# Fetching one edge tile in forty row by row from SyncE and ScalarE in a relational graph network on one core

## The chip, the cores and the metric

The program runs on one core of a Trainium2 chip. The metric is the time of one execution on the device in microseconds (us). The kernel before the change was run three times: 4817.36, 4808.80 and 4808.24 us, median 4808.8 us. The first of these runs is the profiled one.

The engines are called by the profile's names: PE (TensorE, the matrix unit; PEld is its loading of weights), DVE (VectorE), ACT (ScalarE), POOL (GpSimd) and SP (SyncE). SP, ACT and POOL each have a queue from which they issue transfers (DMAs).

## The reference

A graph has 12,500 nodes with 128 features each and 200,000 edges, sorted by destination. The relation of an edge is the place of the greatest of ten numbers in its attributes. A layer takes, for every destination node and every relation, the mean of the features of the source nodes, multiplies each mean by that relation's 128x128 matrix, adds over the relations, and adds a dense term of the node's own features:

```python
def _rgcn_layer(x, src, dst, edge_type, w_rel, root, bias):
    seg = dst * NUM_REL + edge_type
    xs = x[src]
    sums = segment_sum(xs, seg, N * NUM_REL)
    cnt = segment_sum(ones, seg, N * NUM_REL)
    mean = (sums / maximum(cnt, 1.0)[:, None]).reshape(N, NUM_REL, -1)
    return einsum('nrd,rdo->no', mean, w_rel) + x @ root + bias

edge_type = argmax(msg[:, 16:-16], axis=1)
h = relu(_rgcn_layer(x, src, dst, edge_type, w_rel1, root1, b1))
out = layernorm(x + _rgcn_layer(h, src, dst, edge_type, w_rel2, root2, b2))
```

So both layers have to fetch, for each of the 200,000 edges, a row of 128 floats (512 bytes) that an index picks from a table in device memory: the input `x` in the first layer, the hidden table `hD` in the second.

## The kernel before, in words

**Tiles, quads, groups.** The edges are cut into 1563 tiles of 128. Four tiles (`Q`) make a quad and sixteen (`G`) a group, so a layer has 391 quads and 99 groups (the last ones are shorter).

**One quad** (`edges`). POOL fetches the rows of four tiles with one indirect DMA each into a buffer `g` (`gather`, L352); the pool of these buffers has `RING = 22` slots, so POOL can be 22 quads, 88 tiles, ahead. For each tile, DVE builds a matrix `oh` (L366) that holds an edge's weight at the column of its destination and relation, out of 12 destinations by 10 relations, and PE multiplies the rows by it into the accumulator memory `zp` (L368; three buffers of one quad). ACT copies a full `zp` to `zs` (L369; two buffers of one group). DVE has twelve buffers for `oh`.

**One group.** When the four quads of a group are in `zs`, PE multiplies them by the ten relation matrices into `po` (L373), for which there is one buffer (`ps_o`, `bufs=1`). DVE loads the sixteen first destinations into registers, four with one load (L376), and adds each tile's twelve columns to the accumulator `acc` at an address from a register (L381).

**What runs between the quads.** After each quad the function `between` is called. In the first layer it advances the preparation of the next chunks of 128 tiles: types, keys, and `count`, which counts for every edge the edges with the same key among its neighbours at up to `L = 40` places. `count` loads the keys with their neighbours into `kh`, copies them with ACT into accumulator memory as `kp` (L255; pool `ps_k`, one bank), and then compares, for each of 40 distances, a slice of `kp` with a slice of `kh` on DVE (L259), 40 comparisons for a chunk and 13 chunks. PE adds up the results (L260, L261).

**Blocks.** Whenever the groups have passed the end of 512 nodes, `finish` completes that block: `hidden` in the first layer, `final` in the second. Their loads and stores go by SP (`rows_dma`, L287).

**Order.** The program is unrolled. A planner draws up one list for each engine, and an engine works its list in order. A wait stands before the instruction that needs it, so all that is queued on that engine behind a waiting instruction waits too.

Of the kernel before, what the change touches and what calls it, by code (L numbers as in the profile page):

```python
# [9 lines left out]
F32 = mybir.dt.float32  # L10
BF16 = mybir.dt.bfloat16
I32 = mybir.dt.int32
AF = mybir.ActivationFunctionType
ALU = mybir.AluOpType
AX = mybir.AxisListType
PSUM = bass.MemoryType.PSUM
DRAM = bass.MemoryType.DRAM
DVE = mybir.EngineType.DVE
SP = mybir.EngineType.SP

P = 128
NREL = 10
# [3 lines left out]
KW = NREL * WN  # L26
Q = 4
G = 16
RING = 22
L = 40  # L30
CT = 128
YB = 512
# [8 lines left out]
def rgcn_resnorm_kernel(ctx: ExitStack, tc: tile.TileContext, x, src, dst, attr, w_rel1, root1, b1,  # L41
# [13 lines left out]
    nc = tc.nc  # L55
    N, C = x.shape
    E = src.shape[0]
    D = attr.shape[1]
    CE = CT * P
    NT = -(-E // P)  # L60
# [16 lines left out]
    fast = ctx.enter_context(ExitStack())  # L77
# [2 lines left out]
    msgp = fast.enter_context(tc.tile_pool(name="msgp", bufs=2))  # L80
    eqp = fast.enter_context(tc.tile_pool(name="eqp", bufs=6))
    gpool = fast.enter_context(tc.tile_pool(name="gpool", bufs=RING))
    dpool = fast.enter_context(tc.tile_pool(name="dpool", bufs=12))
    zpool = fast.enter_context(tc.tile_pool(name="zpool", bufs=2))
    ps_z = fast.enter_context(tc.tile_pool(name="ps_z", bufs=3, space=PSUM))
    ps_o = fast.enter_context(tc.tile_pool(name="ps_o", bufs=1, space=PSUM))
    ps_k = fast.enter_context(tc.tile_pool(name="ps_k", bufs=1, space=PSUM))
    ps_c = fast.enter_context(tc.tile_pool(name="ps_c", bufs=1, space=PSUM))

    ident = const.tile([P, P], F32, name="ident")  # L90
# [1 line left out]
    idxE = keep.tile([P, NCH * CT], I32, name="idxE")  # L92
# [3 lines left out]
    def chunk_rows(c):  # L96
        return min(CT, NT - c * CT)
# [11 lines left out]
    def to_edges(to, t, c):  # L109

        p = chunk_rows(c)
        pt = ps_c.tile([P, P], F32, name="pt")
        nc.tensor.transpose(pt[:, :p], t[:p], ident[:p, :p])
        nc.vector.tensor_copy(to[:, c * CT:c * CT + p], pt[:, :p])
# [130 lines left out]
    def count(c):  # L245

        p = chunk_rows(c)
        n = p - 1 if c == NCH - 1 else p
        kh = prep.tile([P, P + 2 * L], F32, name="kh")
        nc.sync.dma_start(kh[:n], bass.AP(KD.tensor, KD.offset + c * CE, [[P, n], [1, P + 2 * L]]))  # L250
        if n < p:
            nc.sync.dma_start(kh[n:p], bass.AP(KD.tensor, KD.offset + E - P, [[P, 1], [1, P + 2 * L]]))
        yield
        kp = ps_k.tile([P, P + 2 * L], F32, name="kp")
        nc.scalar.activation(kp[:p], kh[:p], AF.Copy)  # L255
        pc = ps_c.tile([P, P], F32, name="pt")
        for d in range(1, L + 1):
            eq = eqp.tile([P, P + L], BF16, name="eqb")
            nc.vector.tensor_tensor(eq[:p, :P + d], kp[:p, L - d:L + P], kh[:p, L:L + P + d], op=ALU.is_equal)  # L259
            nc.tensor.matmul(pc[:p], identb[:p, :p], eq[:p, :P], start=(d == 1), stop=False)  # L260
            nc.tensor.matmul(pc[:p], identb[:p, :p], eq[:p, d:d + P], start=False, stop=(d == L))  # L261
            if d % 2 == 0:
                yield
        wp = prep.tile([P, P], F32, name="wp")
        nc.vector.tensor_scalar(wp[:p], pc[:p], 1.0, None, op0=ALU.add)
        nc.vector.reciprocal(wp[:p], wp[:p])
        if c == NCH - 1:
            nc.vector.tensor_tensor(wp[:p], wp[:p], own[:p], op=ALU.mult)
        to_edges(wE, wp, c)
        yield  # L270
# [75 lines left out]

    HELD = "clamped to a node on the chip"

    def gather(table, t0, n):
        g = gpool.tile([P, Q, C], F32, name="g")  # L350
        for j in range(n):
            nc.gpsimd.indirect_dma_start(out=g[:, j, :], out_offset=None, in_=table,  # L352
                                         in_offset=bass.IndirectOffsetOnAxis(ap=idxE[:, t0 + j:t0 + j + 1], axis=0))
        return g

    def edges(table, l, t0, n, between):

        zs = zpool.tile([P, NREL, G, WN], F32, name="zs")
        for q in range(0, n, Q):
            m = min(Q, n - q)  # L360
            g = gather(table, t0 + q, m)
            zp = ps_z.tile([P, Q, KW], F32, name="zp")
            for j in range(m):
                t = t0 + q + j
                oh = dpool.tile([P, KW], F32, name="oh")
                nc.vector.tensor_scalar(oh, iota[:, :KW], keyE[:, t:t + 1], wE[:, t:t + 1], op0=ALU.is_equal,  # L366
                                        op1=ALU.mult)
                nc.tensor.matmul(zp[:, j, :], g[:, j, :], oh, start=True, stop=True)  # L368
            nc.scalar.activation(zs[:, :, q:q + m, :], zp[:, :m].rearrange("c j (r n) -> c r j n", n=WN), AF.Copy)  # L369
            between()  # L370
        po = ps_o.tile([P, G, WN], F32, name="po")
        for r in range(NREL):
            nc.tensor.matmul(po[:, :n], wsb[l][:, r, :], zs[:, r, :n], start=(r == 0), stop=(r == NREL - 1))  # L373
        for j0 in range(0, n, 4):
            m = min(4, n - j0)
            _, offs = nc.values_load_multi_w_load_instructions(  # L376
                bt[0:1, t0 + j0:t0 + j0 + m], engines=[DVE], min_val=0, max_val=N - 1,
                skip_runtime_bounds_check_because=HELD)
            for j in range(m):
                s = ds(offs[j], WN)  # L380
                nc.vector.tensor_tensor(acc[:, s], acc[:, s], po[:, j0 + j], op=ALU.add)  # L381

    def groups():
        t = 0
        while t < NT:
            n = min(G, NT - t)
            if n < G and n > 4:
                n = 8 if n > 8 else 4
            yield t, n
            t += n  # L390

    def layer(table, l, finish, steps):

        done = 0
        for t0, n in groups():
            def between():
                while steps:
                    till, left, s = steps[0]
                    k = max(1, -(-left[0] * Q // max(Q, till - t0)))
                    for _ in range(k):  # L400
                        left[0] -= 1
                        if next(s, steps) is steps:
                            steps.pop(0)
                            break
                    break
            edges(table, l, t0, n, between)
            while done < NBLK and (t0 + n >= NT or t0 + n >= (done + 1) * (YB // 8) + SLACK):
                finish(done)
                done += 1
# [5 lines left out]
    def as_steps(f, c):  # L415
        f(c)
        yield
# [5 lines left out]
    for _ in count(0):  # L423
        pass
    todo = []
    for c in range(1, NCH):
        s = [as_steps(sources, c + 1), types(c + 1)] if c + 1 < NCH else []
        todo.append((c * CT - 8, [8 + L // 2 + 2], chain(*s, count(c))))
    layer(x, 0, hidden, todo)
    layer(hD, 1, final, [])  # L430

    pf = ps_f.tile([P, YB], F32, name="pf")
# [19 lines left out]
    def each_tile(before, stages):  # L452

        with tc.For_i(0, E, GT) as e:
# [29 lines left out]
            nw = nc.values_load(bw[0:1, 1:2], min_val=1, max_val=-(-N // W), skip_runtime_bounds_check_because=HELD)  # L484
            b0 = nc.values_load(bw[0:1, 0:1], engines=[DVE, SP], min_val=0, max_val=N - 1,
                                skip_runtime_bounds_check_because=HELD)
# [109 lines left out]
```

## Time and profile before

| | |
|---|---|
| median of three runs | 4808.8 us |
| the profiled execution | 4817.36 us, of it the span of the engines 4815.5 us |
| POOL | busy 2971.9 us (62%), 3126 gathers |
| PE / PEld | busy 2439.3 us (51%) / 2184.5 us (45%) |
| DVE | busy 1585.0 us (33%) |
| ACT | busy 470.9 us (10%) |
| mean granted TensorE clock | 0.706 |
| mean traffic | 58 GB/s |

The span falls into four parts: some 110 us in which the first chunks are prepared while POOL is gathering already; the first layer to about 2346 us; a short change of tables, in which POOL waits 74.2 us for the last rows of `hD`; and the second layer to the end. A busy share is an average over all of it. "Idle before" in a row of the profile is the time in which an engine stood still just before instructions of that group, with the releaser that ended most of it; "issue" is time in which it waited for nothing that the profile shows, "remote" a release whose sender it does not show. Issuing a transfer and loading or computing an address in a register are work of an engine's sequencer and are not in its busy time.

### The profile page before, as it was taken

What the parts mean: (1) busy time and instruction counts of PE and PEld (TensorE: products, weight loads), DVE (VectorE), ACT (ScalarE), POOL (GpSimd) and SP (SyncE); (2) the same over time, 40 slices, a digit from 0 to 9 for tenths busy, and PEclk for the clock granted to TensorE, in tenths of its full rate; (3) what the DMA queues carried; (4) which work ended last, traced back from release to release, by engine and by line L of the source; (5) the groups of instructions that cost most, each with busy time, mean ns of one, the idle gap of its engine ahead of it and who ended that gap; (6) DMA issues with size and microseconds to landing.
All of it is one profiled execution on the core that took longest, in us unless ns stands there. A gap on an engine that the chain in (4) does not pass through costs nothing.

```text
span 4815.5 us, 44360 instructions
## 1 busy us (share of the span) xinstructions
PE 2439.3 (51%) x12272; PEld 2184.5 (45%) x12272; DVE 1585.0 (33%) x7623; ACT 470.9 (10%) x899; POOL 2971.9 (62%) x3136
## 2 busy tenths in 40 slices
PE   0456655655655565665615444444444444444456
PEld 0445554545555455555514443444444444444445
DVE  3333443344334333333302222232222322232234
ACT  0001110111011111111100100000000000000001
POOL 6566666666666666666266666666666666666661
PEclk9766676676767676666756677777777776776777
DMA  5121222122122221112111221112111211121110
GB/s 163 41 75 51 79 76 75 53 76 75 51 80 74 56 55 52 50 51 54 32 48 46 55 53 49 49 52 55 50 51 51 57 51 50 50 56 49 51 52 25
DMA packets 180408, 279.04 MB, mean 58 GB/s; under 512 B 55448, under 2 KB 127015, under 8 KB 177031
## 3 DMA queue, kind: packets, MB, share of 16 engines
q0 software_dynamic: 100032, 205.07, 16.2%
q1 hardware_dynamic: 76957, 69.59, 4.6%
q8 instruction: 108, 1.77, 0.2%
q10 hardware_dynamic: 3168, 1.44, 0.1%
q14 instruction: 143, 1.17, 0.1%
HBM read 262.28 MB, written 13.60 MB: 57 GB/s over the span
## 4 chain that ended last, share of the span: by engine, by line
PE 29%; issue 27%; another core or an unknown queue 24%; DVE 8%; POOL 7%; ACT 2%; DMA 1%; DVEq 1%; SPq 0%; ACTq 0%; POOLq 0%
PE zp L368 14%; PE po L373 12%; POOL g L352 7%; DVE oh L366 4%; DVE acc L381 3%; ACT zs L369 1%; PE pf L303 1%; PE pt L261 1%; PE pt L260 1%; PE pf L302 1%; DMA g<-in_x_dram,idxE 1%; DVEq L376 1%; ACT fT L299 0%; PE pf L297 0%
## 5 line engine op out<-in xcount | busy, mean ns | idle before, releaser
L352 POOL DMA_INDIRECT g<-hD,idxE x1563 | 1477.4, 945 | 946.9 <-issue 429.4
L368 PE MATMUL zp<-oh,g 128*128 128x120 f32 x6252 | 1269.8, 364 | 1551.8 <-issue 1001.8
L352 POOL DMA_INDIRECT g<-in_x_dram,idxE x1563 | 1493.2, 955 | 802.9 <-issue 416.1
L368 PEld LDWEIGHTS zp<-oh,g 128*128 128x128 f32 x6252 | 1134.9, 267 | 1675.4 <-issue 1105.0
L366 DVE TENSOR_SCALAR oh<-iota,keyE,wE 128x120 f32<-128x120 f32 x3126 | 1028.5, 351 | 675.4 <-remote 340.8
L381 DVE TENSOR_TENSOR acc<-acc,po 128x12 f32 x3126 | 518.1, 166 | 2032.6 <-remote 1268.1
L373 PE MATMUL po<-zs,w 128*128 128x192 f32 x3960 | 916.7, 386 | 439.6 <-issue 225.3
L373 PEld LDWEIGHTS po<-zs,w 128*128 128x128 f32 x3960 | 807.2, 232 | 507.5 <-issue 301.7
L369 ACT ACTIVATE zs<-zp 128x480 f32<-128x480 f32 (+1 forms) x782 | 417.8, 570 | 3650.1 <-remote 2408.5
L259 DVE TENSOR_TENSOR eqb<-kp,kh 128x129 bf16<-128x129 f32 (+43 forms) x520 | 148.4, 305 | 196.5 <-remote 145.3
L260 PE MATMUL pt<-eqb,identb 128*128 128x128 bf16 (+1 forms) x520 | 120.9, 269 | 160.0 <-issue 130.7
L261 PE MATMUL pt<-eqb,identb 128*128 128x128 bf16 (+1 forms) x520 | 121.6, 275 | 52.6 <-issue 49.7
L261 PEld LDWEIGHTS <-identb 128*128 128x128 bf16 (+1 forms) x520 | 62.8, 121 | 176.2 <-issue 170.3
L302 PE MATMUL pf<-root,fT 128*128 128x128 f32 x392 | 105.3, 359 | 55.9 <-issue 41.0
L303 PE MATMUL pf<-ident,a 128*128 128x128 f32 x392 | 107.4, 365 | 13.9 <-issue 8.1
L302 PEld LDWEIGHTS pf<-root,fT 128*128 128x128 f32 x392 | 84.3, 263 | 63.9 <-issue 48.0
L260 PEld LDWEIGHTS <-identb 128*128 128x128 bf16 (+1 forms) x520 | 66.8, 129 | 75.4 <-issue 74.9
L303 PEld LDWEIGHTS pf<-ident,a 128*128 128x128 f32 x392 | 88.2, 270 | 22.5 <-issue 14.5
L299 ACT ACTIVATE fT<-pf 128x512 f32<-128x512 f32 (+1 forms) x50 | 29.3, 587 | 498.7 <-remote 245.3
L332 DVE TENSOR_TENSOR v<-pf,xb 128x512 f32<-128x512 f32 (+2 forms) x26 | 17.1, 660 | 174.7 <-remote 127.3
L297 PE MATMUL pf<-ident,hb 128*128 128x128 f32 x98 | 21.9, 356 | 23.9 <-DVE v L332 17.6
L342 DVE TENSOR_SCALAR o<-v,mv,rstd 128x128 f32<-128x128 f32 x98 | 27.8, 349 | 0.2
(71 smaller groups left out, 371.6 us busy)
## 6 DMA issues: line engine op xcount, KB each, us to landing
m<-in_edge_attr_dram SPq DMA_DIRECT2D x24, 1344.0 KB
g<-in_x_dram,idxE POOLq DMA_INDIRECT x1563
g<-hD,idxE POOLq DMA_INDIRECT x1563
xb<-in_x_dram SPq DMA_DIRECT2D x48, 256.0 KB
hD<-hb SPq DMA_DIRECT2D x24, 256.0 KB
hb<-hD SPq DMA_DIRECT2D x24, 256.0 KB
out_dram<-o SPq DMA_DIRECT2D x24, 256.0 KB
w<-in_L_gnn_w_rel_dram ACTq DMA_DIRECT2D x2, 640.0 KB
```

The source lines that it names most:

```text
L259: nc.vector.tensor_tensor(eq[:p, :P + d], kp[:p, L - d:L + P], kh[:p, L:L + P + d], op=ALU.is_equal)
L260: nc.tensor.matmul(pc[:p], identb[:p, :p], eq[:p, :P], start=(d == 1), stop=False)
L261: nc.tensor.matmul(pc[:p], identb[:p, :p], eq[:p, d:d + P], start=False, stop=(d == L))
L302: nc.tensor.matmul(pr[:h, t, :], fT[:, t * P:t * P + h], rsb[l], start=True, stop=False)
L303: nc.tensor.matmul(pr[:h, t, :], a[:, t * P:t * P + h], ident, start=False, stop=True)
L352: nc.gpsimd.indirect_dma_start(out=g[:, j, :], out_offset=None, in_=table, in_offset=bass.IndirectOffsetOnAxis(ap=idxE[:, t0 + j:t0 + j + ...
L366: nc.vector.tensor_scalar(oh, iota[:, :KW], keyE[:, t:t + 1], wE[:, t:t + 1], op0=ALU.is_equal, op1=ALU.mult)
L368: nc.tensor.matmul(zp[:, j, :], g[:, j, :], oh, start=True, stop=True)
L369: nc.scalar.activation(zs[:, :, q:q + m, :], zp[:, :m].rearrange("c j (r n) -> c r j n", n=WN), AF.Copy)
L373: nc.tensor.matmul(po[:, :n], wsb[l][:, r, :], zs[:, r, :n], start=(r == 0), stop=(r == NREL - 1))
L376: _, offs = nc.values_load_multi_w_load_instructions(bt[0:1, t0 + j0:t0 + j0 + m], engines=[DVE], min_val=0, max_val=N - 1, skip_runtime_b ...
L381: nc.vector.tensor_tensor(acc[:, s], acc[:, s], po[:, j0 + j], op=ALU.add)
```

## The change

Of every 80 tiles, one is now fetched by SP and one by ACT in place of POOL. The first layer's SP tiles are 79, 159, ..., ACT's 119, 199, ..., nineteen each in a layer. For such a tile the 128 indices are first loaded into one partition (`sr`); then, eight rows at a time, eight indices are loaded into registers of the engine and eight transfers of 512 bytes are issued, each from a table address that a register holds into one partition of a tile `rows`. One such step of eight rows is taken after a quad, so a tile takes sixteen of the twenty quads that 80 tiles are. Its first rows are issued after the quad that lies eighteen before its own, its last after the quad that lies three before. `gather` skips those tiles, but a quad's buffer keeps its size, and the matmul of a skipped tile reads `rows` in place of `g`.

Three more things change. The ring of gathered quads has 20 slots in place of 22 (80 tiles). The copy `kp` and its bank are gone: both inputs of the 40 comparisons are slices of `kh`. And `ps_o` has two buffers in place of one, so that a group's `po` need not wait until the additions of the group before have read theirs.

```diff
-RING = 22
+RING = 20
+M = 80
+RB = 8
...
+    rpool = fast.enter_context(tc.tile_pool(name="rpool", bufs=2))
...
-    ps_o = fast.enter_context(tc.tile_pool(name="ps_o", bufs=1, space=PSUM))
-    ps_k = fast.enter_context(tc.tile_pool(name="ps_k", bufs=1, space=PSUM))
+    ps_o = fast.enter_context(tc.tile_pool(name="ps_o", bufs=2, space=PSUM))
...
-        kp = ps_k.tile([P, P + 2 * L], F32, name="kp")
-        nc.scalar.activation(kp[:p], kh[:p], AF.Copy)
...
-            nc.vector.tensor_tensor(eq[:p, :P + d], kp[:p, L - d:L + P], kh[:p, L:L + P + d], op=ALU.is_equal)
+            nc.vector.tensor_tensor(eq[:p, :P + d], kh[:p, L - d:L + P], kh[:p, L:L + P + d], op=ALU.is_equal)
...
+    by_rows = {}
+
+    def fetch(table, engine, eng, tag, tiles):
+
+        step = 0
+        for t in tiles:
+            while step < (t - M) // Q + 2:
+                step += 1
+                yield
+            lo = min(t * P, E - P)
+            sr = rpool.tile([1, P], I32, name="sr" + tag)
+            eng.dma_start(sr, src[lo:lo + P].rearrange("(o e) -> o e", o=1))
+            r = by_rows[t] = rpool.tile([P, C], F32, name="rows" + tag)
+            for e in range(0, P, RB):
+                loads, at = nc.values_load_multi_w_load_instructions(
+                    sr[0:1, e:e + RB], engines=[engine], min_val=0, max_val=N - 1,
+                    skip_runtime_bounds_check_because="sources are nodes")
+                for ld in loads:
+                    tc.keep_in_program_order(ld)
+                for i in range(RB):
+                    eng.dma_start(r[e + i:e + i + 1, :], table[ds(at[i], 1), :])
+                step += 1
+                yield
+
     def gather(table, t0, n):
         g = gpool.tile([P, Q, C], F32, name="g")
         for j in range(n):
-            nc.gpsimd.indirect_dma_start(out=g[:, j, :], out_offset=None, in_=table,
-                                         in_offset=bass.IndirectOffsetOnAxis(ap=idxE[:, t0 + j:t0 + j + 1], axis=0))
+            if t0 + j not in by_rows:
+                nc.gpsimd.indirect_dma_start(out=g[:, j, :], out_offset=None, in_=table, in_offset=(
+                    bass.IndirectOffsetOnAxis(ap=idxE[:, t0 + j:t0 + j + 1], axis=0)))
...
-                nc.tensor.matmul(zp[:, j, :], g[:, j, :], oh, start=True, stop=True)
+                rows = by_rows.pop(t) if t in by_rows else g[:, j, :]
+                nc.tensor.matmul(zp[:, j, :], rows, oh, start=True, stop=True)
...
+        fetches = [fetch(table, SP, nc.sync, "s", range(M - 1, NT - 1, M)),
+                   fetch(table, ACT, nc.scalar, "a", range(M + M // 2 - 1, NT - 1, M))]
         for t0, n in groups():
             def between():
+                for f in fetches:
+                    next(f, None)
```

More of the change, by code (lines that the diff above doesn't have):

```diff
@@ L19 @@
 SP = mybir.EngineType.SP
+ACT = mybir.EngineType.Activation
 P = 128
```

## The prediction

> **What bounds the kernel now.** I read the table of busy times first: no engine is full. The fullest, POOL, is busy 2971.9 of 4815.5 us, so some wait between engines sets the end. I then compared stages that do the same work with and without gathers, by the count of PE's `zp` matmuls (two for a tile):
>
> ```profile
> core 0: us, PE busy (x) PEld busy (x) ACT busy (x), PEclk, DMA share, GB/s
> 100.00:2300.00 2200.00, 649.09 (x2972) 552.21 (x2972) 204.20 (x371) 0.69 0.22 62
> 2301.00:2346.00 45.00, 27.45 (x154) 22.81 (x154) 10.84 (x19) 1.00 0.05 13
> 2378.00:4723.00 2345.00, 571.98 (x2963) 540.36 (x2962) 190.43 (x368) 0.70 0.19 52
> 4725.00:4770.00 45.00, 18.28 (x156) 17.52 (x155) 9.21 (x18) 0.96 0.05 13
> ```
>
> The reader is to see 2200 us for 1486 tiles, 1.48 us a tile, and 2345 us for 1481, 1.58 us; but in the two short stretches after a layer's last gather 45 us for 77 tiles, 0.58 us. The chain of PE, DVE and ACT is thus able to run at 0.58 us, and does not while POOL gathers. Yet it does not lack rows. The list of waits says who waits for whom:
>
> ```profile
> engine line waited for: us in total, times, longest us
> ACT zs L369 <- remote: 2408.5, 204, 78.5
> DVE acc L381 <- remote: 1268.1, 112, 54.3
> ...
> POOL g L352 <- PE zp L368: 479.2, 124, 6.1
> PE zp L368 <- ACT zs L369: 459.3, 50, 18.9
> ...
> POOL g L352 <- remote: 196.4, 101, 14.7
> ...
> PE po L373 <- DVE acc L381: 188.1, 84, 15.0
> ...
> PE zp L368 <- DMA g<-hD,idxE: 16.0, 15, 5.9
> ```
>
> PE waits 16.0 us for gathered rows in the second layer; POOL waits 479.2 us for PE to free a slot of the full ring. The timeline shows what the "remote" waits are:
>
> ```profile
> 3193.18 3.52 PE L373 MATMUL po<-zs,w 128*128 128x192 f32 x20 [0.91 <-DVE acc L381]
> ...
> 3205.85 0.94 POOL L352 DMA_INDIRECT g<-hD,idxE  x1 [0.30 <-issue]
> 3206.74 0.37 DVE L381 TENSOR_TENSOR acc<-acc,po 128x12 f32 x2 [13.38 <-remote]
> 3206.80 1.49 ACT L369 ACTIVATE zs<-zp 128x480 f32<-128x480 f32 x3 [18.10 <-remote]
> ```
>
> PE's `po` is recorded as ending at 3196.70, and DVE and ACT, which wait for it, go on together at 3206.74, while POOL gathers one tile every 1.25 us without a break. PE's results reach the others late as long as POOL works. Why, the trace doesn't say. I model it by two rates. In 2378 to 4723 POOL worked 1472.8 us, and 1559 gaps of 0.30 us before a gather make 468: 1941 us, so it stood still for 404. At 0.58 us a tile these 404 us gave 697 tiles; the other 784 took 1941 us, 2.5 us each. A microsecond of gathering that goes away then saves 1 - 0.58/2.5 = 0.77 us (an estimate from these rows).
>
> **The change part by part.**
>
> *Fewer gathers.* 19 + 19 tiles in each of two layers are 76 gathers of 0.95 + 0.30 us: 95 us of POOL. By the factor above, -73 us. Bounds: 0, if the chain is slow for another reason, and -95.
>
> *Row transfers.* 76 tiles of 128 rows are 9728 transfers, half on SP, half on ACT, with 1216 register loads of eight and an address for each row. No transfer at an address from a register runs before. Nearest rows: a transfer with a fixed address occupies SP 0.35 us (median of L104; the shortest of all 0.23), ACT 0.39 to 0.95 (L168, L171); on DVE a load of four registers takes 0.34 us (L376), an address 0.07 (L381). I take 0.40 + 0.07 for a row on ACT, the low end of ACT's own rows, since a row is one short run, and 0.34 for the load: 8 x 0.47 + 0.34 = 4.1 us a step (bounds 8 x 0.30 + 0.34 = 2.7, 8 x 1.02 + 0.34 = 8.5). ACT has 19 x 16 x 2 = 608 steps: 2.5 ms on an engine that is busy 0.47. Behind a step stands the next `zs`, for which PE waits (three `zp` buffers), and for PE then POOL. Before, a `zs` took 0.57 us at once. In the some 4700 us of the layers a result finds ACT inside a step 53% of the time and waits 2.05 us: 1.1 us on average. I charge it at the 225 waits in which POOL stood still for PE or an unseen releaser (124 + 101), since there the chain decides: +248 us. Low bound 0: all hidden while PE's results are late anyway. High bound +600: where three `zs` become ready together, as at 3206.80, the second and third come 4.1 and 8.2 us late, 8.2 us x 198 groups x 0.8 = 1300, about half of it beside the late results. On SP the same steps stand before block loads and stores (L287); those are 130 in all and SP idles beyond, so nothing.
>
> Here a rule of the Trainium skill and the rows differ. "DMA: Bandwidth & Descriptors", section Issuing engines are not separate DMA queues, calls the sequencer's time to start a DMA "usually small relative to the DMA itself"; by it the +248 is near 0 and the sum -113. The rows of SP and ACT, 0.35 us and more a transfer for eight transfers a step, speak against it, and I go by them.
>
> *Comparisons from `kh` twice.* 520 operations at 0.305 us before; with both inputs in SBUF, `bad` (L233, 128 wide) takes 0.28. On DVE nothing. But gathers grow beside such operations:
>
> ```profile
> 991.70 0.81 DVE L182 TENSOR_TENSOR eq<-m,top 128x640 f32<-128x640 f32 x1
> 992.68 0.81 DVE L183 TENSOR_TENSOR eq<-eq,riota 128x640 f32<-128x640 f32 x1
> 995.99 0.82 DVE L182 TENSOR_TENSOR eq<-m,top 128x640 f32<-128x640 f32 x1
> 996.85 0.82 DVE L183 TENSOR_TENSOR eq<-eq,riota 128x640 f32<-128x640 f32 x1
> ```
>
> ```profile
> 991.00 0.94 POOL L352 DMA_INDIRECT g<-in_x_dram,idxE  x1 [0.30 <-issue]
> 992.24 1.08 POOL L352 DMA_INDIRECT g<-in_x_dram,idxE  x1 [0.30 <-issue]
> 996.12 1.51 POOL L352 DMA_INDIRECT g<-in_x_dram,idxE  x1 [0.30 <-issue]
> ```
>
> 1.08 is 0.14 over 0.94 for 0.91 us of overlap, 1.51 is 0.57 over for 1.47: 0.15 to 0.39 per us. 159 us of comparisons overlap gathers 76% of the time: 18 to 47 us of POOL, by 0.77 +14 to +36. I take +25; bounds 0 and +47. "SBUF — State Buffer", section Who interferes with whom, has the rule: a DVE operation with two SBUF inputs contends with a GpSimd operation that reads SBUF, and the loser blocks fully. By it a comparison costs POOL up to its own length, 520 x 0.305 = 159 us, by the factor +122; these rows show less.
>
> *The copy `kp`.* 13 copies of 0.35 us on ACT go; its longest wait, 97.7 us, lies before the layers. Nothing, with -40 (its other waits) as bound.
>
> *Two `po` buffers.* PE waits 188.1 us at `po` for DVE's additions; that goes. But `po`'s result then meets the delay seen at 3206.74, so I take a third: -65 (bounds 0 and -188). Late next is the `zs` slot that `po` frees.
>
> *Ring of 20.* 80 tiles of lead at 1.5 us are 120 us; PE waits 16 us for rows. Nothing while the lead is above a few tiles; if that cover went, POOL's 14.7 us longest wait is the price of one.
>
> Sum: -73 + 248 + 25 + 0 - 65 = +135. The profiled execution took 4817.4 us (span 4815.5 and 1.9 around it), 8.6 above the median: 4817.4 + 135 - 8.6 = 4944, say 4940 us.
>
> **The rivals.**
>
> *ACT's steps stay hidden; faster.* For: ACT is 10% busy and waits 2408.5 us; during gathering PE gives a quad every 10 us, a step is 4.1. Against: POOL's standstills are the time in which progress is made, and ACT is in them. It decides if less than 113 us of the 248 are paid. All hidden: 4809 - 73 + 25 - 65 = 4696, say 4695 us.
>
> *The two queues hold each other up; slower.* POOL's gathers wait for earlier gathers to land (15.8 us, 52 times). If rows of ACT wait so for rows of SP, ACT stands behind SP's stores, and SP waits long at L287 (1018.4 us for ACT's `hb` alone, longest 152.3). If each of 50 blocks holds `zs` 10 us more: 4940 + 500, less the 135 already partly counted, about 5300 us. Against: SP's long waits are mostly idle time with nothing behind.
>
> *POOL isn't relieved.* If rows come later than a gather would have, PE waits for them in place of POOL's ring; three quads, 18 us, lie between the last row and its use, so this needs a step of over 5 us. Its time lies within the first two cases.
>
> **How the numbers follow.** ACT's steps paid: 0.45, 4940, own range 4830 to 5200. Hidden: 0.38, 4695, range 4600 to 4795. Queues: 0.12, 5300. Sums cancel: 0.05, 4809. Slower 0.45 + 0.12 = 0.57, faster 0.38, same 0.05; 0.2%, about 10 us, is what this kernel's measurement can tell from none. The range 4640 to 5280 leaves out a fifth of the faster case below and half of the queue case with the tail of the first above.
>
> **What would show it.** Right: ACT's `zs` stands behind transfers, PE's wait for `zs` grows from 459.3 us, a step takes near 4.1 us; PE's wait at `po` for `acc` is gone; first-layer gathers beside L259 exceed 0.95 us. Wrong: POOL's standstill stays near 676 us and the tile pace falls under 1.48 and 1.58 us, or a step takes under 2.7 us.

## The result and the profile after

The changed kernel takes 5935.6 us (median of 6 runs, 5906.18 to 5952.09) beside 4812.74 us for the kernel before on the same chip: a ratio of 1.2326, 95% interval 1.2291 to 1.2361. The forecast was 4940 us with a range up to 5280. The direction was as forecast; the size, +1123 us against +135, lies far outside the range.

Of the lines named here, those from the gathers on are later by 26 or 27 in the changed kernel: the gathers are now L378, the row transfers L370, `zp` L395, `zs` L396, `po` L400, `acc` L408. The groups of instructions (busy time, mean ns of one, idle time just before them and what ended it):

```profile
L378 POOL DMA_INDIRECT g<-hD,idxE x1525 | 1442.2, 946 | 1472.7 <-PE zp L395 884.9
L378 POOL DMA_INDIRECT g<-in_x_dram,idxE x1525 | 1468.8, 963 | 1412.7 <-PE zp L395 739.5
...
L396 ACT ACTIVATE zs<-zp 128x480 f32<-128x480 f32 (+1 forms) x782 | 438.6, 569 | 4603.4 <-DMA rowsa<-in_x_dram 1067.0
...
L395 PE MATMUL zp<-oh,rowss 128*128 128x120 f32 x76 | 27.2, 459 | 237.3 <-DMA rowss<-hD 106.2
```

The gathers before:

```profile
L352 POOL DMA_INDIRECT g<-hD,idxE x1563 | 1477.4, 945 | 946.9 <-issue 429.4
...
L352 POOL DMA_INDIRECT g<-in_x_dram,idxE x1563 | 1493.2, 955 | 802.9 <-issue 416.1
```

POOL has 76 gathers fewer, as planned, and idles before them for 1472.7 + 1412.7 = 2885 us, the 0.30 us gaps included, where it idled 946.9 + 802.9 = 1750 before. The list of waits says for whom:

```profile
engine line waited for: us in total, times, longest us
POOL g L378 <- PE zp L395: 1624.4, 270, 22.5
...
PE zp L395 <- ACT zs L396: 1103.6, 169, 43.7
ACT zs L396 <- DMA rowsa<-in_x_dram: 1067.0, 144, 33.4
...
ACT zs L396 <- DMA rowsa<-hD: 939.5, 130, 22.3
...
ACT zs L396 <- remote: 502.1, 46, 77.8
```

These rows show the chain. POOL's wait for PE grew from 479.2 to 1624.4 us, PE's wait for the eviction `zs` from 459.3 to 1103.6, and what stood before `zs`, once an unseen releaser for 2408.5 us, is now a row transfer for 1067.0 + 939.5 us. (Such a row means that the last release seen before the eviction was a landing that a row transfer ahead of it in ScalarE's queue waited for; another 319.6 + 279.7 us are put down to the landing of SyncE's rows in the same way.) The stages, by PE's `zp` matmuls alone (two for a tile):

```profile
core 0: us, PE busy (x) PEld busy (x) ACT busy (x), PEclk, DMA share, GB/s
100.00:2850.00 2750.00, 567.26 (x2944) 506.16 (x2944) 204.97 (x365) 0.64 0.18 51
2930.00:2970.00 40.00, 7.84 (x46) 6.99 (x46) 5.04 (x9) 0.70 0.03 8
3050.00:5850.00 2800.00, 584.05 (x3028) 524.80 (x3028) 212.27 (x379) 0.62 0.16 43
```

1.87 and 1.85 us a tile, where 1.48 and 1.58 were. Even in the stretch without a gather (the middle row) a tile takes 40 / 23 = 1.74 us, where it took 0.58: nine evictions in 40 us are one every 4.4 us, the length of one row step. The timeline shows a step at its worst:

```profile
4004.58 0.57 ACT L396 ACTIVATE zs<-zp 128x480 f32<-128x480 f32 x1 [5.47 <-DMA rowsa<-hD]
...
4005.71 14.50 ACTq L370 DMA_DIRECT2D rowsa<-hD  x9
...
4013.76 0.95 POOL L378 DMA_INDIRECT g<-hD,idxE  x1 [0.30 <-issue]
4020.25 0.57 ACT L396 ACTIVATE zs<-zp 128x480 f32<-128x480 f32 x1 [15.11 <-DMA rowsa<-hD]
...
4020.88 1.63 PE L395 MATMUL zp<-oh,g 128*128 128x120 f32 x6 [13.61 <-ACT zs L396]
...
4022.78 0.94 POOL L378 DMA_INDIRECT g<-hD,idxE  x1 [8.08 <-PE zp L395]
```

Nine row transfers hold ScalarE's queue for 14.50 us, `zs` comes 15.11 us after the last one, PE then goes on after 13.61 us and POOL after 8.08. In the instruction records of this stretch the three instructions of a row (an address operation, a register move and the transfer's start, normally 37, 29 and 228 ns) take about 700 ns each or start 0.70 us apart. From 4017.04 us on, 2.3 us after POOL's last gather has ended, they take 37, 29 and 228 ns again, within the same step. A step (from its register load to the end of its eighth transfer) has a median of 5.66 us and a mean of 7.43 us on ScalarE, and 7.82 us mean on SyncE; 46 and 47% of the steps take over 6 us.

### The profile page after: what moved, and what is told of

Its sections match the earlier page's. It is cut to its first block, busy times and chain, and to the rows that moved or that the text cites. A ratio compares the mean times of both kernels' runs of the same rounds, so it can differ in the third digit from the quotient of the medians.

```text
span 5904.3 us, 75298 instructions
## 1 busy us (share of the span) xinstructions
PE 2461.9 (42%) x12272; PEld 2257.6 (38%) x12272; DVE 1709.2 (29%) x7623; ACT 487.1 (8%) x886; POOL 2912.3 (49%) x3060
## 5 line engine op out<-in xcount | busy, mean ns | idle before, releaser
L378 POOL DMA_INDIRECT g<-hD,idxE x1525 | 1442.2, 946 | 1472.7 <-PE zp L395 884.9
L378 POOL DMA_INDIRECT g<-in_x_dram,idxE x1525 | 1468.8, 963 | 1412.7 <-PE zp L395 739.5
L395 PE MATMUL zp<-oh,g 128*128 128x120 f32 x6100 | 1173.6, 350 | 1943.8 <-ACT zs L396 1103.6
L395 PEld LDWEIGHTS zp<-oh,g 128*128 128x128 f32 x6100 | 1048.9, 255 | 2052.5 <-ACT zs L396 1147.4
L392 DVE TENSOR_SCALAR oh<-iota,keyE,wE 128x120 f32<-128x120 f32 x3126 | 1050.3, 353 | 2078.0 <-PE zp L395 1131.5
L400 PE MATMUL po<-zs,w 128*128 128x192 f32 x3960 | 981.0, 420 | 738.1 <-ACT zs L396 452.4
L400 PEld LDWEIGHTS po<-zs,w 128*128 128x128 f32 x3960 | 927.1, 260 | 776.2 <-ACT zs L396 471.2
L408 DVE TENSOR_TENSOR acc<-acc,po 128x12 f32 x3126 | 523.9, 168 | 1700.3 <-PE po L400 965.8
L396 ACT ACTIVATE zs<-zp 128x480 f32<-128x480 f32 (+1 forms) x782 | 438.6, 569 | 4603.4 <-DMA rowsa<-in_x_dram 1067.0
L260 DVE TENSOR_TENSOR eqb<-kh 128x129 bf16<-128x129 f32 (+43 forms) x520 | 132.6, 306 | 180.5 <-remote 110.6
L395 PE MATMUL zp<-oh,rowss 128*128 128x120 f32 x76 | 27.2, 459 | 237.3 <-DMA rowss<-hD 106.2
L395 PEld LDWEIGHTS zp<-oh,rowss 128*128 128x128 f32 x76 | 18.7, 304 | 244.2 <-issue 195.4
```

What stands on the lines that cost most here:

```text
L260: nc.vector.tensor_tensor(eq[:p, :P + d], kh[:p, L - d:L + P], kh[:p, L:L + P + d], op=ALU.is_equal)
L395: nc.tensor.matmul(zp[:, j, :], rows, oh, start=True, stop=True)
```

## The experiments

Theory 1: row steps are stretched while POOL gathers, and an engine that issues rows becomes the bound. Theory 2: the two queues hold each other up through the completion semaphores they share. Theory 3: the rest of the change (the comparisons' operand, the ring, the second `po` buffer) costs it. Ratios are to the kernel before on the same chip; that kernel's own time is given with each set, because it turned out to differ.

### Set 1, kernel before 4792.06 us: the parts of the change

No row fetches:

```
-        fetches = [fetch(table, SP, ...), fetch(table, ACT, ...)]
+        fetches = []
```

> The changed kernel with all 76 row-fetched tiles given back to the indirect gathers; ring of 20, comparisons from kh twice and two po buffers stay. Theory (the row transfers cost the 1123 us): the time falls back to that of before, 4740 to 4840 us; the prediction's own terms for what is left are +25 and -65, so 4770. Rival (the lost PSUM copy, the two-buffer comparisons or the shorter ring cost it): at least 5300 us.

4920.77 us, 1.0265 (1.0248 to 1.0282). The row transfers carry the bulk of the loss, but what is left is 129 us slower than before, not faster.

The same with one `po` buffer:

```
-        fetches = [fetch(table, SP, ...), fetch(table, ACT, ...)]
+        fetches = []
-    ps_o = fast.enter_context(tc.tile_pool(name="ps_o", bufs=2, space=PSUM))
+    ps_o = fast.enter_context(tc.tile_pool(name="ps_o", bufs=1, space=PSUM))
```

> As the kernel without row fetches, and with one po buffer instead of two. The prediction held the second buffer worth 65 us (0 to 188): then this is 65 us above the kernel with two buffers. Rival (PE's wait at po only moves to the next wait, zs or the gathers): within 15 us of it. Against the kernel before it differs only in the comparisons' operand and the ring of 20: the prediction's +25 (0 to 47) should show as 4812 + 25.

4789.99 us, 0.9994 (0.9983 to 1.0004). So the comparisons from `kh` twice, the missing copy `kp` and the ring of 20 are worth nothing together, and the second `po` buffer costs 131 us here, the other sign from the forecast. PE's waits, with two buffers:

```profile
engine line waited for: us in total, times, longest us
PE zp L395 <- DVE oh L392: 574.5, 194, 16.9
PE po L400 <- issue: 500.9, 132, 14.3
```

and with one:

```profile
engine line waited for: us in total, times, longest us
...
PE zp L395 <- ACT zs L396: 542.5, 58, 15.1
...
PE po L400 <- DVE acc L408: 144.2, 71, 9.9
...
PE zp L395 <- DVE oh L392: 47.6, 14, 10.7
```

The wait of 144.2 us at `po` is gone, and a wait of 574.5 us for `oh` has come for one of 47.6. The lists show why it could: they aren't the same. With one buffer the planner puts a group's `po` matmuls behind the first 8 tiles of the next group (49 of 98 groups of the first layer) or behind the first 28 (89 in the second), much as in the kernel before (60 and 89); with two buffers it puts them right behind the group's own last `zp` (97 and 92 groups). `acc` stands before later `oh` operations in DVE's list and waits for `po`'s result, so a late `po` result then holds `oh`, and `oh` holds PE.

SyncE's rows alone, ScalarE's tiles given back to the gathers:

```
-        fetches = [fetch(table, SP, ...), fetch(table, ACT, ...)]
+        fetches = [fetch(table, SP, nc.sync, "s", range(M - 1, NT - 1, M))]
```

> The changed kernel with ScalarE's 38 tiles given back to the gathers; SyncE fetches its 38. Theory 1 (what costs is ScalarE's row steps standing before the PSUM evictions): SyncE's rows stand before nothing that PE waits for, so 4730 to 4850 us. Theory 2 (SyncE and ScalarE hold each other up through the eight completion semaphores that their transfers share): no second queue, 4730 to 4850 as well. Rival (row transfers slow the chip wherever they are issued, or PE waits for rows that come late): 5200 us or more.

5982.82 us, 1.2503 (1.2478 to 1.2528): more than the whole change. Both theories, as I had put them, missed; the rival, in which PE waits for rows that come late, is what came. PE's waits in this run:

```profile
engine line waited for: us in total, times, longest us
...
PE zp L395 <- DMA rowss<-hD: 566.1, 17, 53.8
PE zp L395 <- DMA rowss<-in_x_dram: 272.4, 14, 47.1
PE pf L298 <- DMA hb<-hD: 205.5, 11, 40.3
PE pf L298 <- DMA xb<-in_x_dram: 196.2, 11, 39.3
```

PE waits 838 us for rows that come too late, and 402 us for block loads (6 us in the kernel before) that stand behind rows in SyncE's queue. The 608 steps take 8.36 us on average, 5085 of 5972 us; from its first to its last row a tile takes 152.8 us. At 80 tiles for each such tile, 152.8 / 80 = 1.91 us a tile, times 3126 tiles is 5970 us (an estimate from these figures): SyncE's own rate is the time. The two waits, 838 + 402 us, are about the 1191 us that this run is longer than the kernel before.

ScalarE's rows alone:

```
-        fetches = [fetch(table, SP, ...), fetch(table, ACT, ...)]
+        fetches = [fetch(table, ACT, nc.scalar, "a", range(M + M // 2 - 1, NT - 1, M))]
```

> The changed kernel with SyncE's 38 tiles given back to the gathers; ScalarE fetches its 38. Theory 1 (ScalarE's own issuing, stretched by the gathers, stands before the evictions): most of the loss stays, 5600 to 5900 us. Theory 2 (ScalarE waits for SyncE's rows through shared completion semaphores): without SyncE's rows a step is again about 4 us and the time is below 5150 us.

5553.39 us, 1.1599 (1.1580 to 1.1618), a step of 7.55 us on average. Against the kernels without row fetches that is 633 us (two `po` buffers) to 763 us (one). ScalarE's part of theory 1 holds; of theory 2 nothing is needed: each queue alone has long steps, and the two together cost less than SyncE alone (why less, these runs don't show). SyncE's row transfers do wait for ScalarE's to land, but in the changed kernel's trace for 59.8 us in all, of steps that sum to 4757 us.

### Set 2, kernel before 4932.96 us: the rate of a queue, and the relief of POOL

The 76 tiles neither gathered nor fetched, one `po` buffer:

```
+    def left_out(t):
+        return M - 1 <= t < NT - 1 and t % (M // 2) == M // 2 - 1
...
-            if t0 + j not in by_rows:
+            if not left_out(t0 + j):
...
-                rows = by_rows.pop(t) if t in by_rows else g[:, j, :]
+                rows = pre if left_out(t) else g[:, j, :]
...
-        fetches = [fetch(table, SP, ...), fetch(table, ACT, ...)]
+        fetches = []
```

> One po buffer, no row transfers, and the 76 tiles that the change takes from POOL aren't gathered at all: their matmuls read one preset tile, so the sums of these tiles are left out of the result. PE's list is that of the kernel before. Set against the kernel without row fetches and with one po buffer (0.9994 of before), it is the value of the relief alone. The prediction held it worth 73 us (76 x 1.25 us by a factor of 0.77; 0 to 95): ratio 0.984. Rival (PE's chain is the limit and POOL's gathers don't slow it): within 10 us of before.

4824.25 us, 0.9775 (0.9752 to 0.9798). PE's list has `po` where the kernel without row fetches and with one `po` buffer has it, in all but one of 198 groups (17 differ from the kernel before). Against that kernel's 0.9994, from another chip of this kind, it is 2.2%, about 105 us of 4809: the relief is real and, by this comparison of two chips, worth 1.4 us a gather, more than the 1.25 us that a gather takes with its gap.

SyncE's rows at fixed addresses:

```
-            sr = rpool.tile([1, P], I32, name="sr" + tag)
...
-                loads, at = nc.values_load_multi_w_load_instructions(...)
-                for ld in loads:
-                    tc.keep_in_program_order(ld)
...
-                    eng.dma_start(r[e + i:e + i + 1, :], table[ds(at[i], 1), :])
+                    eng.dma_start(r[e + i:e + i + 1, :], table[e + i:e + i + 1, :])
...
+        fetches = [fetch(table, SP, nc.sync, "s", range(M - 1, NT - 1, M))]
```

> SyncE's 38 tiles, rows at fixed addresses in place of the sources' own: no list of sources, no register loads, no address arithmetic, so this fetches other rows than the reference wants; as many transfers of one row as with SyncE alone before. Theory 1 (each instruction of SyncE's sequencer takes up to 0.70 us while POOL gathers, a row is three or more of them, so a tile takes 150 us of SyncE against 124 us in which 80 tiles pass): one instruction a row is at most 90 us a tile, SyncE keeps up, and the time is 4750 to 4950 us. Theory 2 (the transfers themselves or their shared completion semaphores are slow): no change, 5800 to 6000 us.

5058.81 us, 1.0262 (1.0239 to 1.0286). As many transfers of one row, and the loss falls from 25% to the 1.0265 of the kernel without row fetches. (As a ratio to set 1's 4792.06 us, the expected 4750 to 4950 us are 0.99 to 1.03.) So the transfers, their landing and their semaphores alone don't make the loss; what this edit takes away does: the register loads, the address operations and moves, and the pinned order. It takes them away together, so which share each has isn't told apart: nothing pins the rows here, and the planner spreads them more freely. PE's list isn't that of the kernel without row fetches either (`po` right behind its own group in 31 groups of the first layer, there in 97), so that the two ratios agree so closely is partly luck.

SyncE's rows as in the change, for every 160th tile:

```
-M = 80
+M = 160
...
-        fetches = [fetch(table, SP, ...), fetch(table, ACT, ...)]
+        fetches = [fetch(table, SP, nc.sync, "s", range(M - 1, NT - 1, M))]
```

> SyncE alone with one tile of every 160 (18 in all), rows at the sources' addresses as in the change. Theory 1 (SyncE's own rate is the limit: 150 to 230 us a tile): 160 tiles pass in 250 us, SyncE keeps up, and the time is that without row fetches, 4880 to 4960 us, though half the rows are still fetched so. Rival (each fetched tile costs a fixed price, 1062 us for 38 of them): half the loss, about 5450 us.

5102.99 us, 1.0348 (1.0316 to 1.0380). The steps are no shorter (10.54 us on average, 288 of them, 3036 us), but SyncE now has time for them: half the rows cost 0.8% over the kernel without any (1.0265, on set 1's chip), not half of 22%. The expected 4880 to 4960 us are 1.018 to 1.035 of set 1's 4792.06, so it lies at the upper end. These two points fit a bound: a row step on SyncE costs little until the steps' sum passes the time there is, and from then on it sets the end.

ScalarE's rows at fixed addresses, the same edit with ScalarE alone:

> ScalarE's 38 tiles, rows at fixed addresses (other rows than the reference wants), no register loads or address arithmetic. Theory 1 (a step of eight rows takes 4.2 us where POOL is idle and 7.5 us on average, since each instruction is stretched while POOL gathers, and the step stands before an eviction that PE waits for): a step falls to 2 to 5.6 us, and the loss of 632 us against the kernel without row fetches falls by at least half: 5000 to 5250 us. Theory 2 (the landing of ScalarE's transfers, not their instructions, is what the evictions wait for): 5450 to 5600 us.

4862.02 us, 0.9866 (0.9846 to 0.9885). Expected was that at least half of the loss would go; all of it went, and the time lies below the expected range. Between two evictions the rows now take 3.23 us on average where they took 6.02 with register addresses. The reservation on unpinned rows holds here too (6.5 rows between two evictions on average, in place of 7.5).

### Sets 3 to 5, kernel before 4017.57, 4015.06 and 4019.80 us: other chips

The next set fell on a chip on which the kernel before takes 4018 us, and so did the two after it, on two more chips. Sets 1 and 2 and the result were on chips with 4792 to 4933 us. Five sets, five chips, the three of 4018 us the later ones in time: whether it belongs to the chip or to the hour can't be told from these runs.

The change as it is, on the chip of set 4:

> The changed kernel as it is, on the chip of this set of runs. The kernel before took 4792 and 4933 us on the chips of the first two sets and 4018 us on the chip of the third, where its waiting engines went on less than 1 us after PE's result each time. Theory 1 (gathers hold up the sequencers, where a chip shows it): on a chip on which the kernel before takes about 4800 us, a ratio of 1.22 to 1.25 and steps of 7.5 us on average; on one of 4018 us, steps of 4.2 us, and a ratio of 0.97 to 1.05. Rival (the row transfers are slow of themselves): 1.2 or more on either.

3957.88 us, 0.9855 (0.9838 to 0.9871): here the change is a gain. The timeline of a step:

```profile
2702.44 0.55 ACT L396 ACTIVATE zs<-zp 128x480 f32<-128x480 f32 x1
...
2703.16 4.19 ACTq L370 DMA_DIRECT2D rowsa<-hD  x8
2703.60 0.95 POOL L378 DMA_INDIRECT g<-hD,idxE  x1 [0.30 <-issue]
...
2707.36 0.95 POOL L378 DMA_INDIRECT g<-hD,idxE  x1 [0.30 <-issue]
2707.39 0.57 ACT L396 ACTIVATE zs<-zp 128x480 f32<-128x480 f32 x1 [4.40 <-DMA rowss<-hD]
```

Eight rows in 4.19 us, while POOL gathers without a break: on the result's chip nine took 14.50. Steps against the number of gathers that began in the 7 us before them, from the traces (steps with one to four gathers lie between; in the result's trace they are 398 on ScalarE, 7.56 us on average, 46% over 6):

```
kernel, engine                     no gather: steps, mean us, over 6 us     5 or more: steps, mean us, over 6 us
the change, result, ScalarE             105, 4.66,  9%                          105,  9.72, 86%
the change, result, SyncE               114, 5.62, 27%                          111, 10.27, 80%
ScalarE alone, set 1, ScalarE            69, 4.83, 13%                          153, 10.02, 75%
SyncE alone, set 1, SyncE               247, 4.52,  3%                          149, 12.14, 95%
the change, set 4, ScalarE                1, 5.43,  0%                          590,  4.79,  8%
the change, set 4, SyncE                  1, 4.38,  0%                          591,  4.86,  8%
```

On the chips of the result and of set 1 a step is long when POOL gathers; on that of set 4 the gathers make no such difference. Of the result's 31 long steps on SyncE without a gather before them, each has one that began during the step.

It shows instruction by instruction too. In the result's trace 575 of the 2468 address operations of SyncE that began within 1.3 us of a gather's start took over 300 ns, and 7 of the 1930 that began more than 3 us after the last one (ScalarE: 270 of 2586, and 6 of 1840); in set 4 none of 4864 did on either queue. So a queue on such a chip isn't slow of itself: in one and the same trace it has its usual pace where POOL has paused. Whether the gather's instruction or its transfers hold it up, these counts don't tell.

The same split is in PE's results: an `oh` that had to wait starts more than 2 us after the `zp` it waits for in 284 of 381 cases in the kernel before, and in none of 698 here, where all start within 1 us.

No row fetches, and the same with `po` pinned eight tiles late in PE's list:

```
+        mm = nc.tensor.matmul(po[:, :n], wsb[l][:, r, :], zs[:, r, :n], ...)
+        if r == 0:
+            tc.keep_in_program_order(mm)
...
```

(`po` and `acc` of a group are written behind the next group's second quad. Of the five expectations that follow, the first is for the kernel without row fetches, the others for `po` eight tiles late, except the fourth, for sixteen.)

> The first experiment again (no row fetches, two po buffers, po in the planner's place), as the base of the next kernel on the same chip. On a chip on which the kernel before takes about 4800 us: ratio 1.02 to 1.03; on one of 4018 us, where POOL's 3126 gathers of 1.28 us are the whole time, 0.995 to 1.005.

> As the kernel without row fetches, with po pinned eight tiles late in PE's list. On a chip on which the kernel before takes about 4800 us: by the theory that the order of PE's list costs the 2.65%, 0.985 to 1.00; by the rival that the second buffer itself costs it, 1.02 to 1.03. On one of 4018 us nothing is told apart.

> Without row fetches and with two po buffers, as the first run, but the ten matmuls of a group's po are pinned behind the first eight tiles of the next group in PE's list, where the planner had put them with one buffer in the first layer; with two buffers it had put them right behind their own group's last zp (0 tiles). Theory (the second buffer cost 2.65% because the planner wrote another order for it, in which PE stands at po for the eviction of the group's last quad): the loss goes, ratio 0.985 to 1.000. Rival (the buffer itself, or the lead it gives PE over POOL, costs it): 1.02 to 1.03.

> As the kernel with po eight tiles late, but sixteen tiles late. If PE still stands at po for late evictions at eight, this is below it by some 0.5 to 1.5%; if eight tiles (some 12 us) cover the eviction, within 0.3% of it.

> The kernel without row fetches, two po buffers, po pinned eight tiles late, on another chip. Where the kernel before takes about 4800 us and results come late: by the theory that the order of PE's list costs the 2.65%, 0.985 to 1.00 of the kernel before; by the rival that the second buffer itself costs it, 1.02 to 1.03. Where the kernel before takes about 4016 us: 0.998 again, and the question stays open.

Without row fetches 0.9957 (0.9941 to 0.9974), with `po` eight tiles late 0.9988 (0.9978 to 0.9998) on the same chip, 0.9977 and 0.9984 in sets 3 and 5; sixteen tiles late 0.9985 in set 3. Here the second buffer, in the planner's order, is a gain of 0.4%, and the late order gives most of that back. All these are on chips of 4018 us, where POOL is the bound:

```profile
L378 POOL DMA_INDIRECT g<-in_x_dram,idxE x1563 | 1517.6, 971 | 489.7 <-issue 401.2
L378 POOL DMA_INDIRECT g<-hD,idxE x1563 | 1482.6, 949 | 489.3 <-issue 401.6
```

(no row fetches, set 4): 1517.6 + 489.7 + 1482.6 + 489.3 = 3979 of 4003 us are gathers and their gaps, nearly all of them the 0.30 us that lie before every gather. Whether the list's order is what costs 2.65% on the other kind of chip, as its waits suggest, stays open. One run on such a chip speaks against the buffer itself: ScalarE's rows at fixed addresses have two buffers too and came to 0.9866, and there the planner has put `po` seven or eight tiles late in 31 groups of the first layer and 69 of the second; but that kernel has 38 gathers fewer as well. The change in set 4 has

```profile
L378 POOL DMA_INDIRECT g<-in_x_dram,idxE x1525 | 1517.9, 995 | 478.7 <-issue 409.0
...
L378 POOL DMA_INDIRECT g<-hD,idxE x1525 | 1446.4, 948 | 488.0 <-issue 401.9
```

3931 of 3963 us: POOL is still the bound, and of the 76 gathers at 1.25 us, 95 us, some 41 us arrive, the difference to the kernel without row fetches. Much of the rest goes into the first layer's gathers, 995 ns in place of 971: 37 us for 1525 of them.

Every second tile not gathered (the same `left_out`, `t % 2 == 1 and t < NT - 1`, two `po` buffers):

> No row fetches, two po buffers in the planner's order (the first run's), and every second tile isn't gathered but reads one preset tile, 1562 of 3126 gathers gone; those tiles' sums are left out of the result. Set against the first run's ratio of 1.0265. If a gather costs what the 76 left-out ones did (2.2% for 76, 1.4 us each): -2170 us, 2700 to 2900. By the prediction's two rates (0.58 us a tile without gathers, 0.96 us saved for a gather): -1500 us, 3350 to 3500. If PE's chain were the limit and gathers beside it were free: above 4500 us.

2455.37 us, 0.6112 (0.6102 to 0.6122), in set 3. On a chip whose results come promptly a gather left out saves (4017.57 - 2455.37) / 1562 = 1.0 us on average, PE then being busy 2049.4 of 2448.9 us; my two rates belonged to another kind of chip, and the figures in the expectation can't be held against this.

Row fetches of both queues and no gather at all:

```
-            if t0 + j not in by_rows:
+            if False:
...
-                rows = by_rows.pop(t) if t in by_rows else g[:, j, :]
+                rows = by_rows.pop(t) if t in by_rows else pre
```

> The changed kernel with both queues' row fetches, and no gather at all: the tiles that POOL gathered read one preset tile, so nearly all sums are left out; the row transfers, their registers and their two queues are as in the change. Theory 1 (POOL's gathers stretch every instruction of the two sequencers): no step over 6 us on either engine, median 4.1 to 4.5 us, a tile takes SyncE about 67 us. Theory 2 (the queues hold each other up, or the transfers are slow of themselves): nearly half of the steps stay above 6 us. The time, with ScalarE's 4.2 us a step and 0.6 us an eviction per four tiles in 80% of the layer: 3100 to 3700 us by theory 1, above 4500 by theory 2.

> Row fetches of both queues and no gather, nearly all sums left out, on the chip of this set. On a chip on which the kernel before takes about 4800 us: by theory 1 (gathers stretch the sequencers' instructions) no more than 8% of the steps over 6 us, address instructions 37 and 29 ns, and 3450 to 3650 us as on the other chip; by the rival (this chip's queues are slow in any case) nearly half of the steps over 6 us and above 4500 us.

> Row fetches of both queues and no gather, nearly all sums left out. Where the kernel before takes about 4800 us: by the theory that the gathers stretch the sequencers on such a chip, address instructions of 37 and 29 ns, at most 10% of the steps over 6 us, and 3450 to 3650 us; by the rival that such a chip's queues are slow without gathers too, nearly half of the steps over 6 us and above 4500 us.

3534.53, 3533.12 and 3532.3 us in sets 3 to 5. The step has a median of 4.12 us on SyncE and 4.25 on ScalarE, 3 and 7% over 6 us, address operations 37 and 29 ns. But on these chips the steps are short with gathers too, so nothing is told of the other kind. There the evidence is the table and the counts above, inside single traces; a run without gathers on such a chip is missing.

The run has a use of its own: with no gather, the change's row steps hold the chain to 3533 us, well above the 2455 us with half of the gathers and no rows. On a chip of 4018 us that floor lies under POOL's, so the change can still gain there.

## Why the prediction was wrong, point by point

**What bounds the kernel.** That the chain of PE, DVE and ACT is held up while POOL gathers, and runs at 0.58 us a tile when it doesn't, was read rightly from that trace. That this belongs to some chips only, one trace can't show.

**Fewer gathers, -73 us (0 to -95).** -105 us by leaving them out, where nothing is put in their place: the sign was right, the term too small and past its bound. More came back than the 95 us that the gathers take, which a factor of 0.77, or of 1, can't give, so the two rates aren't the whole mechanism. In the changed kernel it never appears on the result's chip, since POOL had no use for it: it idles 1135 us more than before.

**Row transfers on ACT, +248 us (0 to +600).** This step failed in size. "8 x 0.47 + 0.34 = 4.1 us a step" is right for a step that nothing stretches: 4.3 us median with no gather in the 7 us before it, 4.4 on set 4's chip. On the result's chip the mean is 7.43 us. The trace of before held a warning that I didn't carry over: PE's results were late as long as POOL worked, and I took that lateness for PE's alone, not for anything that ACT's and SP's queues would do. The charge was wrong too. I multiplied a mean wait of 1.1 us by 225 waits; but where nothing else holds the chain, a step before every eviction sets its pace, 1.74 us a tile in the stretch without gathers, in place of 0.58. ScalarE alone cost 633 to 763 us, above the high bound.

**On SP "nothing".** This is the step that failed most. I asked what stands behind SyncE's steps, and not whether SyncE gets through them. Its sum was at hand: 16 steps of 4.1 us are 66 us for each 80 tiles, against 124 us in which 80 tiles pass, so a factor of 1.9 was all the room, and at 8.36 us a step, 134 us, it was gone. SyncE alone cost 25%. In the changed kernel, where ScalarE's steps slow the chain already, its rows add less: 1.2326 against 1.1599 with ScalarE alone in set 1, PE waiting 106.2 + 60.4 us for them.

**The rule against it.** "DMA: Bandwidth & Descriptors" of the Trainium skill, section Issuing engines are not separate DMA queues, calls the time to start a DMA usually small relative to the DMA itself. By it the rows' term is near 0. With SyncE alone (set 1) the steps of 38 tiles, starts with their register loads and address operations, took 5085 of 5972 us, so on such a chip their sum isn't small. On set 4's chip the outcome by it, a gain, has the sign of the 0.9855 measured, though the median step is no less than 4.2 us there.

**Comparisons, copy and ring, +25 + 0 + 0.** 0.9994 (0.9983 to 1.0004): together nothing, within the bounds. The rule of "SBUF — State Buffer", section Who interferes with whom, that the loser of the port blocks fully, would have given +122 us as the prediction applied it; the run excludes that. The prediction had left out that the same section reports `tensor_tensor`, the operation of these comparisons, as not having stalled a DMA in a probe, and with that the run agrees. The first layer's gathers have a mean of 963 ns against 955.

**Two `po` buffers, -65 us (-188 to 0).** Wrong sign on the chip of set 1, +131 us. I took the buffer for the removal of one wait. It also changed what the planner writes, and with it the wait that comes next. In the changed kernel itself `po` stands mostly 8 tiles late again (55 and 52 groups), as ScalarE's steps make the planner hold it back, so these 131 us are no term of its sum. On set 4's chip the second buffer was a gain of 0.4%.

**The rivals.** "POOL isn't relieved" named the case: rows that come later than a gather would have, from a step of over 5 us on. I gave it no time of its own, on the ground that it lay within the first two cases; its condition was met by nearly half of the steps, and with SyncE alone its price was 1062 us (5982.82 against 4920.77). "The two queues hold each other up" isn't needed: each alone has the long steps. "ACT's steps stay hidden; faster", 4695 us or 0.976 of before, has the sign that a chip of 4018 us shows: 0.9855. That the direction came out as forecast is thus in part luck with the chip.

**What would show it.** PE's wait for `zs` grew as named, PE's wait at `po` for `acc` fell from 188.1 to 2.0 us, and POOL's standstill for PE or an unseen releaser, which I had watched only for staying near 676 us, grew to 1624.4 + 150.3 = 1775. First-layer gathers hardly grew.

## What to carry to other kernels

Before giving an idle queue many small instructions, set their sum for one period against the length of that period, with the stretched duration that the trace shows for other engines at such times, and mistrust a small factor: here 1.9 was no room. A transfer of one row at a register's address is three sequencer instructions and a share of a register load; what looks like DMA work is issue work, and it is paid by whatever stands behind it on that engine. When a buffer count changes, compare the instruction lists before costing the wait that it removes, and before trusting a sign, measure on more than one chip.

## What I hadn't expected of the hardware

The same kernel takes 4792 to 4933 us on some chips and 4015 to 4020 us on others. On the first kind, while POOL's indirect gathers run back to back, many instructions of SyncE's and ScalarE's sequencers take about 0.70 us each in place of 37, 29 and 228 ns (12% of SyncE's address operations in the changed kernel lie between 0.6 and 0.8 us, none in set 4), and PE's results reach the waiting engines late, in the kernel before an `oh` by more than 4 us in 190 of its 381 waits. On the second kind neither occurs, with gathers at the same pace of 1.25 us. Not every sequencer is held up: in the changed kernel's trace each of DVE's 3126 address operations takes 69 ns. Single durations of the others aren't to be trusted there, since some address operations last as little as 2 ns, in set 4 none under 37; the sums over steps are. The cause isn't known from these runs. With it goes the difference between a gain of 1.45% and a loss of 23% for one and the same change.
